# Four blocks on one core: the first half group ahead of the rest, its causal mask by a matrix product, fillers in TensorE's pauses, block 4's weights later, and separate buffers for the two feed-forward weights

## The chip, the core and the metric

The kernel runs on one NeuronCore of a Trainium2 chip. A core has TensorE (PE in the profile, with its weight loads as PEld), VectorE (DVE), ScalarE (ACT), GpSimd (POOL) and SyncE (SP), which here issues all DMAs. Each engine works through its own list of instructions in order; semaphores order them against each other. The metric is the device time of one execution in microseconds. Three runs of the kernel before gave 2677.88, 2680.63 and 2684.55, median 2680.63.

## The reference, cut to what matters

The input is x of shape [8, 1024, 256] in f32: 8 sequences of 1024 rows. Four blocks follow each other, each as `x = x + block(layernorm(x))`:

```python
x = x + _L0_attn_ref(_layernorm(x), ...)   # linear attention layer, own FFN 256-1024-256
x = x + _L0_ffn_ref(_layernorm(x), w1, b1, w2, b2)         # relu FFN 256-1024-256
x = x + _L1_attn_ref(_layernorm(x), W_qkv, b_qkv)          # softmax attention, one head
x = x + _L1_ffn_ref(_layernorm(x), w_gate, w_up, w_down)   # gated FFN 704 wide, fp4 inputs
```

Block 1, the linear attention, has 16 heads of 16 columns. With q and k after a sigmoid (so all entries are positive), and cumulative sums along the sequence:

```python
sink_in  = normal / einsum('bhld,bhld->bhl', q + EPS, cumsum(k, 2) + EPS)
src_out  = normal / einsum('bhld,bhld->bhl', k + EPS, cumsum(q, 2) + EPS)
cons_sink = einsum(..., q + EPS, cumsum(k * src_out[..., None], 2) + EPS) / normal
cons_src  = einsum(..., k + EPS, cumsum(q * sink_in[..., None], 2) + EPS) / normal   # then clip, exp
x = einsum('bhld,bhldm->bhlm', qs, cumsum(einsum('bhld,bhlm->bhldm', k, vs), 2)) * sink_alloc[..., None]
```

After it come an output product, a layernorm, a GELU feed-forward net and a second layernorm. In block 4 inputs and weights are quantized to fp4 in blocks of 16 values and widened again before each product.

## The kernel before, in words

**Tiling.** Rows are taken in chunks of 128, four chunks in a group (`G`), two groups in a sequence, so there are 64 chunks and 16 groups. All products are f32. Linear attention works by groups: `linear_group(p)` normalizes four chunks (`front`) and starts `linear_span`, which makes q and k, the running sums (scans on VectorE), the sums over heads (products `prod,hsum`) and `scale`; then `linear_chunk` handles each chunk: the product of k and q (`qz`, PSUM banks of 512 columns for four heads each), the causal mask, the product with v (`sc,v_pad`), the running state `kv`, the output product (`wo,xo`) and layernorm. The first group alone is done as two half groups (`spans` of chunks 0 to 1 and 2 to 3), which spread a packed per-head factor over columns by products with a mask (`spread_near`, tiles `flow` and `scale` times `mask`); all other groups spread it by a DMA to memory and back (`packed`, `spread`).

The causal mask of a chunk is a VectorE multiplication of each bank with an upper triangle, `sc = bank * triu`, four for each chunk.

**Feed-forward nets.** `dense()` runs over the groups; in a group first the GELU net on rows `hT`, then the ReLU net on rows `nT`, each for two halves of 256 rows and eight slices `f` of the 1024 hidden columns. One step is a first product (`half,w_ff`, two matmuls of 256 columns), the activation on ScalarE (`hidden`), and, `LAG = 2` steps later, the second product (`w_ff,hidden`), which adds into a bank of its half. There are 512 such steps. The weights of a step come from memory each time: `load_weights` issues, for each step, one DMA for the slice of the first weight and one for the slice of the second, into the two halves of one buffer `w_ff` of 512 columns; `W_FF = 5` such buffers exist, and one is free again after the second product of its step. After a half's last step `norms_1` or `norms_2` follows.

**Softmax and fp4.** `softmax_and_fp4` starts `soft_chunk` for each chunk of a sequence that is fully through block 2: scores (`n2T,qT`), exp, transposes, value product (`vt,probT`), normalization, fp4 quantization of 256 columns, gate and up products, fp4 quantization of 704 columns, down product (`wdT,hqT`), output DMA. `fp4_weights` quantizes block 4's weights in 18 pieces (`w_raw`) with the same VectorE steps.

**What sets the order.** Every part is a generator that yields what it needs next (engine, tiles, banks, a condition, and `at`, a due time in units of a group). `Plan.run` keeps a model of when each engine and tile is free, and at each turn takes the part with the smallest key: time that TensorE would wait, then how unripe it is, then engine, and last the due time. Instructions are pinned in the order in which they are issued (`Queue.issue`, so nearly all of the profile's instructions bear one line, L331). The order is thus fixed when the program is built; at run time nothing is reordered.

```python
wait = max(max(t) - now - (0.3 if stays else 0.0), 0.0)
unripe = max(t[1] + self.RIPE[queue] - now, 0.0)
key = wait, unripe, queue == "tensor", not stays, part[2]
```

Of the kernel before, what the change touches and what calls it, by code (L numbers as in the profile page):

```python
# [29 lines left out]
G = 4  # L30
# [32 lines left out]
class Plan:  # L63
# [12 lines left out]
    def __init__(self, tc, nc):  # L76
# [17 lines left out]
        self.ran = self.slow = 0.0  # L94
        self.parts = []
# [63 lines left out]
    def took(self, queue, op, args, kw):  # L159
# [13 lines left out]
        if queue == "tensor":  # L173
# [5 lines left out]
            if tiled:  # L179
                cost *= 0.25  # L180
# [80 lines left out]
    def act(self, *tiles, **kw):  # L261
        return self.need("scalar", tiles, **kw)
# [27 lines left out]
    def run(self):  # L290
        while self.parts:
            now = self.free.get("tensor", 0.0)
            best = None
            for part in self.parts:
# [5 lines left out]
                wait = max(max(t) - now - (0.3 if stays else 0.0), 0.0)  # L300
                unripe = max(t[1] + self.RIPE[queue] - now, 0.0)
# [3 lines left out]
            assert best is not None, "every part waits for another"  # L305
            if best[0][0] > 0.0 or best[1][1].queue == "tensor":
                self.free["tensor"] = max(now, best[2])
# [42 lines left out]
def block_stack_kernel(ctx: ExitStack, tc: tile.TileContext, a: dict, out: bass.AP):  # L350
# [138 lines left out]
    mask_tiles = [make("prob", "mask") for _ in range(2)]  # L489
    late = set()  # L490

    def masks():
        yield act(ident, at=0.02)
        for b in range(4):
# [12 lines left out]
    def late_constants():  # L507
# [10 lines left out]
        late.add("hsum")  # L518
        yield dve()
# [153 lines left out]
    def fp4_weights():  # L673
# [15 lines left out]
        for i, (src, turns) in enumerate(pieces):  # L689
            for j in range(i, min(i + 3, len(pieces))):  # L690
                if j not in raws:
# [3 lines left out]
                        dma(at=1.5 + 1.6 * i / len(pieces), when=lambda: count["stage"] == 4),  # L695
# [7 lines left out]
            at = 1.5 + 1.6 * i / len(pieces)  # L703
# [187 lines left out]
    def linear_group(p):  # L891
# [34 lines left out]
        for i in range(G):  # L926
            plan.start(front(i), p + 0.03 * i)
# [19 lines left out]
    def linear_span(p, span, fronts, tiles):  # L947
# [13 lines left out]
        after = 0.25 if span.start else 0.0  # L961
        near = len(span) < G

# [145 lines left out]
    def linear_chunk(p, i, n0T, comp, qk):  # L1109

        s, g = divmod(p, NG)
        past, c = seqs[s]["past"], p * G + i
        here = slice(i * P, (i + 1) * P)
# [6 lines left out]
        for k in range(2):  # L1120
# [25 lines left out]
                at=p + 0.62 + 0.06 * i,  # L1146
# [7 lines left out]
        qz = tile_qz.rearrange("p (k e t) -> p k e t", k=2, e=2)  # L1154
        for e in range(2):
# [4 lines left out]
        yield pe(qz, banks=4, tiled=True)  # L1160
        banks = []
        for r in range(4):
            rows = slice(32 * r, 32 * r + 32)
            bank = mm_bank()
            banks.append(bank)
            for k in range(2):
# [4 lines left out]
                    start=True,  # L1171
                    stop=True,
                )
        plan.drop(tile_qz)
        scores = []
        for bank in banks:
            sc = yield from fresh("flow", dve(bank), "sc")
            sc = sc.rearrange("p (n t) -> p n t", n=4)
            nc.vector.tensor_tensor(
# [7 lines left out]
        if not end:  # L1187
            yield pe(banks=1, at=p + 0.66 + 0.06 * i, when=lambda: count["attended"] == c)
# [77 lines left out]
        yield pe(xo, banks=1, at=p + 0.7 + 0.06 * i, when=lambda: "chunk" in late)  # L1266
        bank = mm_bank()
        for k in range(2):
# [14 lines left out]
            at=p + 0.74 + 0.06 * i,  # L1283
# [373 lines left out]
```

## Time and profile before

| what | before |
|---|---|
| median of three runs | 2680.63 us |
| profiled execution, its own time | 2684.53 us |
| its span, first to last instruction | 2682.8 us |
| PE busy / DVE busy / ACT busy | 2600.5 / 1937.8 / 1253.2 us |
| mean granted TensorE clock | 0.988 |
| VectorE mask `sc<-bank,triu`, 256 times | 160.6 us, 679 ns each |
| first-layer weight and second-layer weight DMAs | 1024 of 128 KB |
| table loads on ACT | 298, 1283 ns each |

Columns of the views: in the windows a line gives start:end of a stretch, its length, then for each engine the busy time and number of instructions, the granted clock as a share of full speed, the DMA engines' share and GB/s. In the timeline a line gives start, duration, engine, source line, operation, the tiles written and read, how many like instructions were merged, and in brackets the idle time just before and what ended it. An f32 product is two records on TensorE. A granted clock of 0.5 means that the same product takes twice as long. In the first 15 us the record of the clock is missing and the column shows 1.00.

### The profile page before, as it was taken

The page shows a single profiled execution, that of the slowest core. Times are in us where ns is not written, and L with a number is a line of the kernel's source. Part 1 is how long each engine was busy: PE and PEld are TensorE (multiplying, and loading weights), DVE is VectorE, ACT ScalarE, POOL GpSimd, SP SyncE. Part 2 cuts the span into 40 slices and gives each one's busy share as a digit, 9 for nine tenths or more (in the row PEclk, how much of TensorE's full clock was granted, in tenths as well). Part 3 has the DMA queues.
Part 4 walks back from the last instruction along what each step waited for, and adds up shares of the span by engine and source line. Part 5 has one row for each costly group of instructions (what it writes and reads, how often), then busy time and mean ns, then how long its engine had stood idle before and what let it go on. Part 6 is the DMA issues. An engine that isn't in the chain of part 4 may idle for free.

```text
span 2682.8 us, 45525 instructions
## 1 busy us (share of the span) xinstructions
PE 2600.5 (97%) x16687; PEld 2020.7 (75%) x16687; DVE 1937.8 (72%) x4368; ACT 1253.2 (47%) x2600; POOL 585.4 (22%) x1101
## 2 busy tenths in 40 slices
PE   6999999999999999999999999999999999999997
PEld 4777777777777877777777777777777777787765
DVE  7788786776858768586776858668586777855565
ACT  3444445546454453544445454453545435445342
POOL 1332222131212213132221212213122221212000
PEclk8899999999999999999999999999999999999999
DMA  3334232322223232232323223132322313222000
GB/s 87 98 107 142 79 95 74 95 70 86 70 81 105 69 87 66 75 107 64 103 62 89 72 77 109 60 89 70 93 77 72 103 58 87 74 75 81 28 16 8
DMA packets 286814, 211.88 MB, mean 79 GB/s; under 512 B 24704, under 2 KB 275072, under 8 KB 286592
## 3 DMA queue, kind: packets, MB, share of 16 engines
q1 hardware_dynamic: 286592, 208.97, 26.7%
q8 instruction: 133, 2.18, 0.3%
q14 instruction: 89, 0.73, 0.1%
HBM read 188.17 MB, written 20.71 MB: 78 GB/s over the span
## 4 chain that ended last, share of the span: by engine, by line
PE 81%; DVE 12%; DMA 3%; ACT 2%; issue 1%; POOL 1%; SPq 0%; DVEq 0%; ACTq 0%; POOLq 0%
PE bank L331 81%; DVE hid L331 1%; DVE prod L331 1%; DMA spread<-packed 1%; DVE n L331 1%; ACT L331 1%; DVE ln_st L331 1%; DVE x_amax L331 1%; DVE div L331 1%; DVE res L331 1%; DVE u L331 1%; DMA packed<-scale 1%; DVE q L331 0%; DVE ln_mv L331 0%; POOL ln_rstd L331 0%
## 5 line engine op out<-in xcount | busy, mean ns | idle before, releaser
L331 PE MATMUL bank<-half,w_ff 128*128 128x256 f32 x2048 | 535.5, 384 | 15.1 <-DMA w_ff<-in_L_ffn_w_dram 7.7
L331 PE MATMUL bank<-w_ff,hidden 128*128 128x256 f32 x2048 | 532.9, 384 | 0.0
L331 POOL TENSOR_SCALAR ln_ve<-ln_mv 128x1 f32<-128x1 f32 x384 | 103.3, 269 | 1747.3 <-DVE ln_mv L331 1739.3
L331 PEld LDWEIGHTS bank<-half,w_ff 128*128 128x128 f32 x2048 | 379.8, 191 | 93.3 <-issue 24.8
L331 PEld LDWEIGHTS bank<-w_ff,hidden 128*128 128x128 f32 x2048 | 370.6, 191 | 88.5 <-issue 39.1
L331 ACT ACT_TABLE_LOAD x298 | 382.3, 1283 | 5.2
L331 ACT ACTIVATE hidden<-bank,c_L_ffn_b 128x256 f32<-128x256 f32 x256 | 120.8, 472 | 298.9 <-PE bank L331 298.9
L331 POOL TENSOR_TENSOR ln_rstd<-ln_ve,neghalf 128x1 f32<-128x1 f32 x384 | 237.5, 619 | 32.0
L331 PE MATMUL bank<-n2T,qT 128*128 128x512 f32 x512 | 242.1, 596 | 1.1 <-ACT qT L331 1.1
L331 PE MATMUL bank<-vt,probT 128*128 128x256 f32 x1024 | 232.0, 380 | 0.0
L331 PEld LDWEIGHTS bank<-vt,probT 128*128 128x128 f32 x1024 | 193.3, 190 | 32.9 <-issue 2.9
L331 ACT ACTIVATE hidden<-bank,c_L_attn_b 128x256 f32<-128x256 f32 x256 | 119.7, 468 | 193.6 <-PE bank L331 192.9
L331 DVE TENSOR_TENSOR hid<-hid,bank 128x352 f32<-128x352 f32 x118 | 60.9, 516 | 199.0 <-PE bank L331 165.4
L331 PE MATMUL bank<-wdT,hqT 128*128 128x256 f32 x768 | 177.8, 381 | 0.8 <-ACT hqT L331 0.8
L331 PE MATMUL bank<-wgT,xqT 128*128 128x352 f32 x512 | 174.9, 464 | 0.6 <-ACT xqT L331 0.5
L331 PE MATMUL bank<-wuT,xqT 128*128 128x352 f32 x512 | 172.4, 459 | 0.0
L331 DVE TENSOR_TENSOR sc<-bank,triu 128x512 f32<-128x512 f32 x256 | 160.6, 679 | 13.0 <-PE bank L331 12.0
L331 PEld LDWEIGHTS bank<-wdT,hqT 128*128 128x128 f32 x768 | 144.5, 191 | 22.9 <-issue 1.7
L331 PEld LDWEIGHTS bank<-n2T,qT 128*128 128x128 f32 x512 | 94.3, 191 | 71.7 <-issue 61.3
L331 PEld LDWEIGHTS bank<-wuT,xqT 128*128 128x128 f32 x512 | 97.5, 190 | 54.5 <-issue 0.5
L331 PEld LDWEIGHTS bank<-wgT,xqT 128*128 128x128 f32 x512 | 95.2, 191 | 36.8 <-issue 1.9
L331 PE MATMUL bank<-ident,n 128*128 128x128 f32 x512 | 93.7, 278 | 21.8 <-DVE n L331 14.5
(213 smaller groups left out, 4363.8 us busy)
## 6 DMA issues: line engine op xcount, KB each, us to landing
w_ff<-in_L_attn_W_dram SPq DMA_DIRECT2D x512, 128.0 KB
w_ff<-in_L_ffn_w_dram SPq DMA_DIRECT2D x512, 128.0 KB
spread<-packed SPq DMA_DIRECT2D x90, 256.0 KB
x<-in_L_attn_inputs_dram SPq DMA_DIRECT2D x64, 128.0 KB
xr<-in_L_attn_inputs_dram SPq DMA_DIRECT2D x64, 128.0 KB
rows<-res SPq DMA_DIRECT2D x64, 128.0 KB
out_dram<-y SPq DMA_DIRECT2D x64, 128.0 KB
rows<-rows SPq DMA_DIRECT2D x56, 128.0 KB
```

Source lines behind the costliest of these rows:

```text
L331: ins = method(*args, **kw)
```

## The change

Six edits.

1. *First half group first.* The parts of chunks 0 and 1 of the first group get due times lowered by 1, which makes them negative; the planner calls a negative due time urgent: such a part counts as ripe at once. `after`, which is added to the due times of a span, becomes -1.0 for the first span of the first group; for the second it stays 0.25.
2. *The mask by a product.* In the first group a bf16 tile `later` holds (triu - 1) times 2 to the 100th, four times over, and an identity. A bf16 product of the two is written to each score bank first, and the scores are added to it; ScalarE's Relu then copies the bank to `sc`. Masked entries come out as zero. This replaces the VectorE multiplication in four chunks, 16 times. `later` takes one of the two `q_c` tiles until the last chunk of the first group is done.
3. *Fillers.* Where the planner's model has TensorE pause for more than 1.6 us, products of the identity with itself are put into the list ahead of the next instruction, one for each 0.22 us of the pause less 0.7.
4. *Block 4's weights later.* The due times of the 18 pieces go from 1.5 + 1.6 i/18 to 2.0 + 2.5 i/18.
5. *Softmax chunks later.* Their due times go from 3 + cc/4 to 3.5 + cc/4.
6. *Separate buffers.* The first weights go to tiles `w_in`, the second to `w_out`, five each of 256 columns, loaded by two generators; a `w_in` is free after its first product, a `w_out` after its second.

```diff
-                wait = max(max(t) - now - (0.3 if stays else 0.0), 0.0)
-                unripe = max(t[1] + self.RIPE[queue] - now, 0.0)
+                wait = max(max(t) - now - (0.3 if stays or part[2] < 0.0 else 0.0), 0.0)
+                urgent = part[2] < 0.0
+                unripe = 0.0 if urgent else max(t[1] + self.RIPE[queue] - now, 0.0)
                 key = wait, unripe, queue == "tensor", not stays, part[2]
                 if best is None or key < best[0]:
                     best = key, part, max(t)
             assert best is not None, "every part waits for another"
+            pause = max(now, best[2]) - self.ran
+            if pause > 1.6 and best[1][1].queue == "tensor" and self.fill is not None:
+                if (self.banks_free(best[1][1].banks + 1) or 0.0) <= self.ran + 0.4:
+                    self.fill(pause - 0.7)
...
+    later = make("q_c", "later")[:, : GT + P]
...
+        nc.scalar.copy(later[:, GT:], ident)
...
+        yield dve(triu)
+        nc.vector.tensor_scalar(
+            later[:, :GT].rearrange("p (n t) -> p n t", n=4),
+            triu.unsqueeze(1).to_broadcast([P, 4, P]),
+            -1.0,
+            2.0**100,
+            ALU.add,
+            ALU.mult,
+        )
...
-                        dma(at=1.5 + 1.6 * i / len(pieces), when=lambda: count["stage"] == 4),
+                        dma(at=2.0 + 2.5 * i / len(pieces), when=lambda: count["stage"] == 4),
...
-            plan.start(front(i), p + 0.03 * i)
+            plan.start(front(i), p + 0.03 * i - (p == 0 and i < 2))
...
-        after = 0.25 if span.start else 0.0
         near = len(span) < G
+        after = 0.25 if span.start else -1.0 if near else 0.0
...
+        at = p - (p == 0 and i < 2)
...
+        by_act = p == 0
         for e in range(2):
             nc.scalar.activation(
                 qz[:, :, e, :], qk[0][:, :, here], AF.Copy, scale=parity[:, e : e + 1]
             )
 
-        yield pe(qz, banks=4, tiled=True)
-        banks = []
-        for r in range(4):
+        yield pe(qz, *([later] if by_act else []), banks=4, tiled=not by_act)
+        banks = [mm_bank() for _ in range(4)]
+        for bank in banks:
+            if by_act:
+                nc.tensor.matmul(
+                    bank, lhsT=later[:, GT:], rhs=later[:, :GT], start=True, stop=False,
+                    skip_group_check=True,
+                )
+        for r, bank in enumerate(banks):
             rows = slice(32 * r, 32 * r + 32)
-            bank = mm_bank()
-            banks.append(bank)
             for k in range(2):
                 nc.tensor.matmul(
                     bank[:, k * D : (k + 1) * D],
                     lhsT=qk[1][rows, k, here],
                     rhs=qz[rows, k, :, :],
-                    start=True,
+                    start=not by_act,
                     stop=True,
+                    skip_group_check=True,
                 )
         plan.drop(tile_qz)
         scores = []
         for bank in banks:
-            sc = yield from fresh("flow", dve(bank), "sc")
+            sc = yield from fresh("flow", (act if by_act else dve)(bank), "sc")
             sc = sc.rearrange("p (n t) -> p n t", n=4)
+            if by_act:
+                nc.scalar.activation(sc, bank.rearrange("p (n t) -> p n t", n=4), AF.Relu)
+                scores.append(sc)
+                continue
...
-        def load_weights():
+        def load_weights(names, used, loaded, first):
+
             ws, n = [], 0
             for p in range(flows):
-                for wa, wb in (("L0_attn_W1", "L0_attn_W2"), ("L0_ffn_w1", "L0_ffn_w2")):
+                for name in names:
                     for f in 2 * list(range(NF)):
                         yield dma(
-                            at=p + 0.9 + n % 32 / 32,
-                            when=lambda: n < W_FF + seconds[0] and count["stage"] >= 2,
+                            at=p + 0.9 + (n % 32 + (0 if first else LAG)) / 32,
+                            when=lambda: n < W_FF + used[0] and count["stage"] >= 2,
                             unused=ws[n - W_FF :][:1] if n >= W_FF else (),
                         )
-                        w = big.tile([P, 2 * D], F32, tag="w_ff", name="w_ff", bufs=W_FF)
+                        tag = "w_in" if first else "w_out"
+                        w = big.tile([P, D], F32, tag=tag, name=tag, bufs=W_FF)
                         cols = slice(f * P, (f + 1) * P)
-                        nc.sync.dma_start(
-                            out=two(w[:, :D]), in_=a[wa][:, cols].rearrange("(k p) n -> p k n", p=P)
-                        )
-                        nc.sync.dma_start(out=w[:, D:], in_=a[wb][cols, :])
+                        if first:
+                            nc.sync.dma_start(
+                                out=two(w), in_=a[name][:, cols].rearrange("(k p) n -> p k n", p=P)
+                            )
+                        else:
+                            nc.sync.dma_start(out=w, in_=a[name][cols, :])
                         ws.append(w)
                         loaded.append(w)
                         n += 1
 
-        loaded, seconds = [], [0]
-        plan.start(load_weights(), 0.9)
+        firsts, seconds = [0], [0]
+        w_in, w_out = [], []
+        plan.start(load_weights(("L0_attn_W1", "L0_ffn_w1"), firsts, w_in, True), 0.9)
+        plan.start(load_weights(("L0_attn_W2", "L0_ffn_w2"), seconds, w_out, False), 0.9)
...
-                        behind.append((p, b, half, f, hidden, w))
+                        firsts[0] += 1
+                        behind.append((p, b, half, f, hidden))
...
-                at=3 + cc / 4,
+                at=3.5 + cc / 4,
...
+    def fill(us):
+
+        bank = mm_bank()
+        while us > 0.0:
+            nc.tensor.matmul(bank[:, :P], lhsT=ident, rhs=ident, start=True, stop=True)
+            us -= 0.22
+        plan.let_go(bank)
+
+    plan.fill = fill
```

## The prediction

> **What bounds the kernel.** I read the page first: busy shares, the slices, the chain that ended last.
>
> ```profile
> PE 2600.5 (97%) x16687; PEld 2020.7 (75%) x16687; DVE 1937.8 (72%) x4368; ACT 1253.2 (47%) x2600; POOL 585.4 (22%) x1101
> ...
> PEclk8899999999999999999999999999999999999999
> ...
> PE 81%; DVE 12%; DMA 3%; ACT 2%; issue 1%; POOL 1%; SPq 0%; DVEq 0%; ACTq 0%; POOLq 0%
> ```
>
> TensorE is the bound, and the chain is mostly TensorE work. But busy is not useful here: the first slices run below full clock. So I asked for busy time by stretch, cut at the first feed-forward product (76), at the transposes of `scale` in the second and third group (149, 256), at the last feed-forward product (2501) and at the last chunk's value product (2641).
>
> ```profile
> 0.00:76.00 76.00, 49.60 (x351) 36.20 (x352) 56.56 (x145) 23.82 (x65) 16.56 (x43) 0.80 0.30 77
> 76.00:149.00 73.00, 68.94 (x488) 54.91 (x488) 56.45 (x120) 30.62 (x74) 22.32 (x41) 0.95 0.41 115
> 149.00:256.00 107.00, 98.53 (x739) 78.47 (x738) 87.67 (x210) 46.60 (x115) 31.12 (x58) 0.94 0.41 119
> 256.00:2501.00 2245.00, 2226.11 (x14443) 1738.67 (x14442) 1623.80 (x3638) 1086.92 (x2214) 508.01 (x940) 1.00 0.28 81
> 2501.00:2641.00 140.00, 132.41 (x581) 95.50 (x579) 92.03 (x218) 57.28 (x117) 6.69 (x18) 0.99 0.05 17
> 2641.00:2683.00 42.00, 24.89 (x92) 16.93 (x90) 21.27 (x42) 7.95 (x16) 0.74 (x2) 0.88 0.03 10
> ```
>
> Columns: length, busy of PE, PEld, DVE, ACT, POOL, granted clock, DMA share, GB/s. Between 256 and 2501 nothing is to be had; the losses lie at the two ends. To size them I priced each product at its start-to-start spacing at full clock (216 ns for a record of 256 columns, two records per product; 109 for a transpose) and counted the records of each stretch. All work comes to 2531 us of the 2683; 152 are lost: 72 before 268 us, 46 between 268 and 2479, 34 after. The timeline shows their kinds:
>
> ```profile
> 49.56 4.14 PE L331 MATMUL bank<-qz,k 32*128 32x256 f32 x32
> ...
> 75.51 1.69 PE L331 MATMUL bank<-half,w_ff 128*128 128x256 f32 x4
> ...
> 129.67 2.07 PE L331 MATMUL bank<-half,w_ff 128*128 128x256 f32 x4 [3.75 <-DMA w_ff<-in_L_ffn_w_dram]
> ...
> 160.10 2.11 PE L331 MATMUL bank<-qz,k 32*128 32x256 f32 x16 [3.73 <-ACT qz L331]
> ...
> 237.22 2.07 PE L331 MATMUL bank<-half,w_ff 128*128 128x256 f32 x4 [3.11 <-DMA w_ff<-in_L_ffn_w_dram]
> ...
> 2674.11 1.51 PE L331 MATMUL bank<-ident,q 128*128 128x128 f32 x6 [7.28 <-DVE q L331]
> ```
>
> Four `half,w_ff` records take 2.07 us after a pause and 1.03 otherwise (90.72): each pause costs itself and some 3.4 us of halved rate. The queue that loads weights shows why two pauses are DMA:
>
> ```profile
> 120.38 0.89 SPq L331 DMA_DIRECT2D w_ff<-in_L_ffn_w_dram  x2
> 121.44 2.55 SPq L331 DMA_DIRECT2D spread<-packed  x4
> 124.09 1.04 SPq L331 DMA_DIRECT2D w_ff<-in_L_ffn_w_dram  x2
> ```
>
> The next pair stands behind `spread`, four transfers of 256 KB, and its product starts only at 129.67.
>
> **What the Trainium skill says.** "TensorE: Matmul & The Clock Gate", part 1 (What's actually happening): the clock is halved after an idle window of about 3.4 us and freed by a busy one, the windows running freely. The trace agrees: 42.5 to 52.8 and 66.4 to 76.7 run at clock 0.50, three windows each. Same page, Back-to-back issue gap: an isolated 512-column single-pass product takes N/2.4 + 2.5, some 216 ns; before has no bf16 product, so this is the only price. "ScalarE: Activation LUTs", Table sets: relu is in every set, so the new Relu should load no table; no run shows it yet.
>
> **The change, part by part.** Sums are made against the profiled execution: span 2682.8, its own time 2684.5; the median, 2680.6, is 3.9 lower.
>
> *Added TensorE work.* 16 mask products at 216 ns: 3.5 us. 141 fillers of 128 columns f32, two records of about 108 ns: 30.5 us at full clock. They cost nothing if they stand in real pauses: that is what must be checked. In the built order they stand in runs of 29, 6, 19, 11, 15 and 18 at the start, 6, 10, 14 and 13 at the end.
>
> *First half group first.* I follow the new order with old durations. `ident` is written by 3.04, so the 29 fillers start at 3.1; the first 3.4 to 6.8 us are at half clock: 6.3 + 1.7 to 3.4 = they end at 11 to 13, where `n` (now ahead of `rpos` and `same` on DVE, ready about 8.5) went through at 9.15. That is 2 to 3 us late, but at full clock: `k` reaches DVE at about 14.5, as before (14.38). Then the old run loses what the new order avoids: `wk` of the second half sat between `flow` and its mask products (22.98 to 26.35 on DVE): 3 us; second-half scans among the first's: 3 us. So first `weighted` at 22.5 (26.35), twelve DVE rows of 7 us and a carry wait of 1 to 30.5, head sums 0.7, `e` at 31.2 (37.51), then 4.7 (5.6 before, with the second half's `r` and `flow` inside): `scale` at about 36 instead of 43.1. At full clock what follows it shrinks (43.28 to 53.64 was half rate): scores out at 41 to 43. Eight Relus at about 0.6 (nearest row: ACT `prob` 128x512, 0.683; DVE's `sc` is 0.679) put attention at 45; `kT`'s copy stands behind seven of them, counted. Then `xo` 46.6, `wo` 47.6, `u` 48.8 (behind five rows of the second half), `h` of chunk 0 at 51; chunk 1's share the queue with 2.5 us of second-half rows: 55.8. The transposes and their copy end near 57: first feed-forward product at 57 against 75.5.
>
> *What that buys.* By the order lists 27.3 us of work precede that product before, 24.6 after. By the second group's `scale` it is 91.0 at 149.2, so 58 lost. After, the work is 94.2, and DVE sets the time: its rows up to there sum to 107.0 before and 107.8 after (16 `sc` of 0.62 gone, four more pieces of block 4's weights come earlier, 2.6 each). With DVE idle 15 us until 57 and 11 later: 134, so 40 lost. Bounds: no later idle 122, its old idle share 142. From there to the third group's `scale` before takes 107.2 for 89.6 of work; after 90.3 of work, no DMA pause (3.1, and 3.4 of halved clock), a shorter wait for `qz` (18 fillers hold the clock) and small waits: 96, bounds 92 and 107. Third `scale` at 230 instead of 256.4: 26 us gained, mask products included; bounds 7 and 42.
>
> *Separate buffers.* The same bytes and issues: five of 512 columns become five and five of 256. A first-layer weight comes free two steps earlier (the lag), 3.5 us at 1.73 a step. In SP's new order five `w_in` of the second network stand ahead of `spread`, three of them ahead of `packed`, where before had one pair, so the pause at 124.9 goes; it lies in the DVE-bound stretch, so it is in the 26, not on top. SP is in order and each `w_out` now waits alone; behind one stand `spread` and `xr`, for which DVE waits, as it did with pairs. Nothing to add.
>
> *Block 4's weights later.* Only the last ones move: the final piece from step 69 of the first products to 92, but eight pieces stand by step 18, where before had three. DVE between the third and fourth `scale` falls from 88 to 72 against TensorE's 108 and 98: hidden. One `q_c` buffer is held for the mask until the first group is done; Square waits behind DVE anyhow.
>
> *15 more table loads* at 1.283: 19 us of ACT, hidden under TensorE (ACT is 47% busy); uncovered, 1.3 us before a hidden tile each.
>
> *End.* Softmax chunks run half a group later; 181 us of work remain after the last feed-forward product against 148. Before, from the last value product's end (2641.1) to the last `y` (2680.0) 38.9 us pass for 19.6 of work, since the last two chunks share DVE and the last products run halved. In the new order the previous chunk's products fill its start: 2.6 + 4.7 of products, 3.0 of fillers, `n` at 10.8, products 4.7 to 16.3, transposes and `wdT` of the previous chunk to 20.3, last quantization 6.7 on DVE to 23.6, then 4.6: 28.2. Gain 10; bounds 5 (fillers 3 us late, one more wait) and 13. The stretch before it lost 11.6 for 128 of work; 162 at the same rate lose 14: 2 back. Middle: 46 lost, 23 of it in pauses under 1.9 us, 8 either way, taken as 0.
>
> Sum: 2684.5 - 26 - 10 + 2 = 2650.5; less 3.9: 2647.
>
> **Rivals.** (1) *DVE gives it back.* More pieces early stand in front of the second group's chain; TensorE runs out of feed-forward steps and waits. For it: DVE is 50 of 67 busy there, and a run of 18 fillers stands before that `scale`. Against: 16 `sc` are gone. Start gains 13, end 4: 2664. (2) *More than the ends.* `w_in` earlier also takes small waits of the middle, DVE without idle: start 36, end 12, middle 6: 2632. Against: DMA is only 0.8 of the waits after 268. (3) *Fillers delay work.* They are in order; one in front of a ready product costs itself. The 98 of the start at half rate are 42 us, the 43 of the end 9: if no pause were there, 2647 + 51 = 2698. It decides when 34 of these 51 hit ready work (no gain), 42 for slower. Against: TensorE idles 26 of the first 76 us. (4) *The clock stays halved* although filled: then only idle is rearranged, 2658; it lies within (1) and the forecast.
>
> **Numbers.** 0.3% (8 us, 2672.6 to 2688.6) is what a measurement tells from no change. Forecast 2647, own range 2636 to 2660: 0.60. (1) 2660 to 2672: 0.18. (2): 0.10. Within 0.3%: 0.05. (3), slower: 0.07. Faster 0.88. The range 2628 to 2668 leaves out half of (2), a third of (1) and the rest.
>
> **What would show it.** Right: first `w_in` product at 52 to 62; second and third `scale` transposes at 128 to 140 and 222 to 240; no `w_in` DMA pause over 2 us before 268; clock near 1.0 from 15 to 160; 28 us from the last value product to the last `y`; middle 46 lost. Wrong: fillers at 3 us ending after 14, products ready behind a run, `sc` Relus over 0.7, or DVE idle with TensorE idle before 250.

## The result, and the profile after

The changed kernel takes 2675.27 us (median of 13 runs, 2673.53 to 2677.35), the kernel before 2683.25 in the same session (13 runs). The ratio is 0.9971, with a 95% interval from 0.9963 to 0.9978: 8 us faster, where 34 had been forecast. The profiled span is 2674.1 us against 2682.8.

From the page of the changed kernel: busy time by engine, the granted clock in 40 slices, and the chain that ended last.

```profile
PE 2616.3 (98%) x16985; PEld 2040.7 (76%) x16985; DVE 1943.5 (73%) x4353; ACT 1282.5 (48%) x2641; POOL 566.3 (21%) x1101
...
PEclk9999999999999999999999999999999999999999
...
PE 67%; DVE 25%; DMA 3%; ACT 2%; issue 2%; POOL 1%; SPq 0%; DVEq 0%; POOLq 0%; ACTq 0%
```

Averaged over each slice, the clock is near full everywhere now. The chain is 67% TensorE where it was 81%, and 25% VectorE where it was 12%. That share says where the chain runs and not that TensorE waits longer: over the whole kernel its waits for VectorE sum to 37.8 us, where they were 56.9. They moved, as will be seen, from the ends into the middle. The same stretches as before (the last one ends with the shorter span):

```profile
0.00:76.00 76.00, 65.64 (x558) 55.81 (x559) 55.06 (x147) 35.78 (x97) 14.07 (x39) 1.00 0.37 93
76.00:149.00 73.00, 67.15 (x504) 52.57 (x503) 64.10 (x147) 32.15 (x76) 26.98 (x47) 0.98 0.42 119
149.00:256.00 107.00, 104.06 (x803) 84.23 (x803) 89.57 (x216) 49.34 (x120) 35.35 (x68) 1.00 0.46 131
256.00:2501.00 2245.00, 2215.32 (x14357) 1726.36 (x14357) 1616.98 (x3581) 1093.15 (x2211) 483.24 (x930) 1.00 0.28 80
2501.00:2641.00 140.00, 136.71 (x628) 100.25 (x627) 100.14 (x230) 66.30 (x127) 5.91 (x16) 1.00 0.05 16
2641.00:2674.00 33.00, 27.43 (x143) 21.50 (x141) 17.67 (x35) 5.73 (x12) 0.74 (x2) 1.00 0.04 13
```

The reader is to see two things. VectorE is busy 64 of the 73 us from 76 to 149 (56 before). And in the middle stretch, where nothing was expected to move, TensorE is busy 11 us less in the same 2245. The lines that answer to those of before, from the timeline of the changed kernel:

```profile
42.05 1.17 PE L337 MATMUL bank<-qz,k 32*128 32x256 f32 x16
...
60.61 1.13 PE L337 MATMUL bank<-half,w_in 128*128 128x256 f32 x4 [0.46 <-ACT half L337]
...
130.38 1.13 PE L337 MATMUL bank<-half,w_in 128*128 128x256 f32 x4
...
163.46 1.17 PE L337 MATMUL bank<-qz,k 32*128 32x256 f32 x16
...
2663.02 3.06 PE L337 MATMUL bank<-ident 128*128 128x128 f32 x26
2666.61 0.87 PE L337 MATMUL bank<-ident,hid 128*128 128x128 f32 x6 [0.53 <-DVE hid L337]
```

The first feed-forward product comes at 60.6 instead of 75.5, the DMA pauses at 129.67 and 237.22 are gone, so is the `qz` pause at 160, and before the last chunk's transposes stand fillers instead of 7.28 us of idle time.

Where the time went is counted as in the forecast. The lost time of a stretch is its length less the price of its TensorE records, and the price of a record is its start-to-start spacing at full clock in the kernel before; fillers count as lost. The stretches are cut at the transposes of `scale` of the third, fifth and sixteenth group.

| lost, us | to 3rd | 3rd to 5th | 5th to 16th | after 16th | two groups, steady |
|---|---|---|---|---|---|
| before | 73.2 | 11.1 | 32.4 | 37.1 | 320.6 |
| changed | 56.8 | 5.2 | 52.5 | 27.2 | 324.6 |

Below, "start" is the first of these columns, "middle" the third and "end" the fourth. The last column is the mean time of two groups between the eighth and the sixteenth. The start gains 16.4, of which the mask products take some 3.4 back: the third `scale` comes at 243.9 instead of 256.4 (230 was forecast). Groups four and five give 6 more, the end gives 10. Then the steady middle takes 20 back. Kernels with the same written order up to the third `scale` lost 55.3 to 58.2 there: a difference of under 3 us in one profile means nothing.

### The profile page after: what moved, and what is told of

Read it like the earlier page. It is cut to its first block, busy times and chain, and to the rows that moved or that the text cites. A ratio compares the mean times of both kernels' runs of the same rounds, so it can differ in the third digit from the quotient of the medians.

```text
span 2674.1 us, 46660 instructions
## 1 busy us (share of the span) xinstructions
PE 2616.3 (98%) x16985; PEld 2040.7 (76%) x16985; DVE 1943.5 (73%) x4353; ACT 1282.5 (48%) x2641; POOL 566.3 (21%) x1101
## 3 DMA queue, kind: packets, MB, share of 16 engines
q1 hardware_dynamic: 286592, 208.97, 27.2%
## 4 chain that ended last, share of the span: by engine, by line
PE 67%; DVE 25%; DMA 3%; ACT 2%; issue 2%; POOL 1%; SPq 0%; DVEq 0%; POOLq 0%; ACTq 0%
PE bank L337 67%; DVE hid L337 4%; DVE prod L337 3%; DVE n L337 2%; DVE ln_st L337 2%; DVE u L337 1%; DMA spread<-packed 1%; DVE x_amax L337 1%; DVE res L337 1%; DVE spread L337 1%; DMA packed<-flow 1%; DVE ln_mv L337 1%; ACT L337 1%; DVE div L337 1%; DVE mx L337 1%
## 5 line engine op out<-in xcount | busy, mean ns | idle before, releaser
L337 PE MATMUL bank<-half,w_in 128*128 128x256 f32 x2048 | 529.7, 381 | 6.7 <-DVE kv L337 3.4
L337 PE MATMUL bank<-w_out,hidden 128*128 128x256 f32 x2048 | 532.4, 383 | 0.0
L337 PEld LDWEIGHTS bank<-w_out,hidden 128*128 128x128 f32 x2048 | 369.8, 190 | 97.1 <-issue 45.1
L337 PEld LDWEIGHTS bank<-half,w_in 128*128 128x128 f32 x2048 | 378.0, 190 | 78.2 <-issue 19.8
L337 DVE TENSOR_TENSOR sc<-bank,triu 128x512 f32<-128x512 f32 x240 | 149.5, 680 | 9.3 <-PE bank L337 7.7
L337 PEld LDWEIGHTS bank<-wgT,xqT 128*128 128x128 f32 x512 | 94.4, 190 | 40.6 <-issue 6.3
L337 DVE TENSOR_TENSOR hid<-hid,q_c 128x704 f32<-128x704 f32 x116 | 102.8, 886 | 2.5
```

The costliest lines, as they stand in the source:

```text
L337: ins = method(*args, **kw)
```

## What cost the middle

Theory 1: the softmax chunks' new due time. Theory 2: the split weight buffers. Theory 3: an order that the new start leaves behind. Each is one part undone in the changed kernel; the due time was also put alone into the kernel before.

**The due time undone.**

```diff
-        at = 3.5 + cc / 4
+        at = 3 + cc / 4        # and at the two places that start a chunk
```

> The changed kernel, softmax chunks due at 3 + cc/4 again instead of 3.5 + cc/4. Theory 1 (the due time that frees the tail puts the softmax chunks of the middle in worse places): groups 5 to 15 lose some 32 us of TensorE time beyond its work, as before, instead of 52; the tail loses 37 again instead of 27; time some 2665. Theory 2 (the split weight buffers cost the middle) and theory 3 (an order inherited from the start does): the middle keeps its 52, the tail loses 37; time 2685.

Measured: 2666.45 us, ratio to before 0.9931 (0.9915 to 0.9948). Middle 35.2, end 32.7, two groups 320.1. Theory 1 holds for the middle; at the end only half of the gain went away. Waits of TensorE between the fifth and the sixteenth `scale`, from the view of waits (total us, times, longest), first the changed kernel, then this one:

```profile
PE bank L337 <- DVE sc L337: 5.6, 6, 1.7
PE bank L337 <- DVE v L337: 3.9, 7, 1.0
PE bank L337 <- DVE res L337: 3.6, 3, 1.2
PE bank L337 <- DVE prod L337: 3.4, 5, 1.2
PE bank L337 <- DVE kv L337: 2.2, 2, 1.1
```

```profile
PE bank L337 <- DVE v L337: 6.0, 9, 1.3
PE bank L337 <- ACT prob L337: 2.6, 5, 0.9
PE bank L337 <- DVE sc L337: 1.7, 1, 1.7
```

These are short waits, under 2 us, for rows (single instructions of VectorE) of the attention (`sc`, `kv`), of the scans (`prod`) and of the norms (`res`). VectorE was at work for 3.3 us or more of the 4 us before every one: the row waited for stands behind other rows. All waits of the view sum to 24.2 us in the changed kernel, 12.1 in the one before and 14.2 here. Counted as spacing over the price, pauses of over 0.25 us sum to 32.7, 14.3 and 16.9, which is nearly the whole difference. They return at fixed distances: the 1.19 us before an `h` transpose at 849.7 come again at 1498.2 and 2147.7. The order that the planner writes repeats, every four groups in the changed kernel, every two in this one.

**The due time alone, in the kernel before.**

> The kernel before with one edit, softmax chunks due at 3.5 + cc/4 instead of 3 + cc/4. Theory A (the later due time lets the written order fall into a repeating order with more pauses at results of VectorE, whatever the rest): the middle loses 40 to 52 instead of 32.4, two groups take over 321.5 us instead of 320.6, the tail loses 31 to 33 instead of 37.1 (it has no fillers): 2687 to 2700. If it takes the new start and the split buffers as well: middle 32, tail 32, 2677 to 2680.

Measured: 2687.15 us, 1.0009 (1.0001 to 1.0018). Middle 47.7 (32.4), end 31.3 (37.1), two groups 323.5. The view of waits between the fifth and sixteenth `scale`:

```profile
PE bank L331 <- DVE v L331: 13.1, 16, 1.7
PE bank L331 <- DVE kv L331: 4.8, 4, 1.2
PE bank L331 <- DVE res L331: 1.2, 1, 1.2
```

The kernel before waits 8.5 us for `v` and not at all for `kv` or `res`. So the later due time costs 15 to 17 us of middle in both kernels, and gains 5 to 6 at the end.

**The weight buffers joined again** (the loader, its two `dma_start` into one `w_ff` of 512 columns, and `w[:, D:]` in the second layer, as before).

> The changed kernel with both layers' weights in one buffer and one loader again. Theory 2 (split buffers cost the middle): the middle loses 32 instead of 52 and the time falls to some 2655 to 2660. Theories 1 and 3: the middle keeps 50 or more, DMA pauses ahead of first-layer products come back in the first 268 us (one or two of 3 us and 3.4 us of halved clock each); time 2675 to 2685.

Measured: 2680.56 us, 0.9984 (0.9976 to 0.9991). Middle 45.8, two groups 323.0; but the start loses 62.6 and groups four and five 11.3. Theory 2 falls: without the split the kernel is slower. The middle does lose 6.7 less than in the changed kernel, but not the 20 that the theory asks for; from the seventh group on the products stand in the order of the kernel without precedence, which comes next. Waits of TensorE before 268 us, this kernel:

```profile
PE bank L337 <- ACT qz L337: 3.8, 1, 3.8
...
PE bank L337 <- DMA w_ff<-in_L_ffn_w_dram: 3.2, 2, 2.9
```

Neither line is there in the changed kernel: the split is what removed both the DMA pause and the `qz` pause.

**The precedence of the first half undone.**

```diff
-            plan.start(front(i), p + 0.03 * i - (p == 0 and i < 2))
+            plan.start(front(i), p + 0.03 * i)
-        after = 0.25 if span.start else -1.0 if near else 0.0
+        after = 0.25 if span.start else 0.0
-        at = p - (p == 0 and i < 2)
+        at = p
```

> The changed kernel without the precedence of the first half group (front, turns and the attention's due times as before); mask by a product, fillers, later weights, split buffers and later softmax stay. Theory 3 (the order that the start leaves behind costs the middle): the middle loses 32 instead of 52 although the first feed-forward product comes at 68 to 76: time 2660 to 2675. Theories 1 and 2: the middle stays at 50 or more and the first product 8 to 15 us later costs 4 to 15: 2679 to 2690.

Measured: 2669.75 us, 0.9942 (0.9927 to 0.9957), faster than the changed kernel. Start 60.1, middle 40.4, two groups 322.2; the second `scale` comes at 142.8 instead of 147.6, although the first feed-forward product is as late as before (75.5). From the second group on, the planner's rules are those of the changed kernel; only what it starts from differs. So theory 3 holds beside theory 1: at one and the same due time the middle falls into different repeating orders.

**Block 4's weights at their old due times** (1.5 + 1.6 i/n).

> The changed kernel with the due times of block 4's weights as before (1.5 + 1.6 i/n instead of 2 + 2.5 i/n). The written order of the first three groups is that of the changed kernel, and so is that of the middle from the tenth group on: start 57, middle 50 to 53, tail 27; only the third to ninth group differ, where more VectorE work may cost up to 6: 2674 to 2681. If the due times matter for the start: outside that.

Measured: 2675.57 us, 0.9966 (0.9952 to 0.9979); start 55.9, middle 51.9, end 27.2. These due times alone change nothing that can be measured.

**Other due times**, 2.5 and 4.

> The changed kernel with softmax chunks due at 2.5 + cc/4. If the middle's loss grows with the due time: two groups take under 320 us, the middle loses 25 to 33, the tail 33 to 38: 2660 to 2668. If 3 is a good place by chance: two groups take 322 to 326, 2672 to 2690.

> The changed kernel with softmax chunks due at 4 + cc/4. If the middle's loss grows with the due time: two groups take over 325 us, the middle loses 55 or more, the tail 22 to 27: 2678 to 2695. If 3.5 is a bad place by chance: two groups take 320 to 323, 2662 to 2672.

Measured: at 2.5 2718.39 us (1.0131, 1.0116 to 1.0146), middle 80.7, two groups 329.1; at 4 2684.18 us (1.0004, 0.9995 to 1.0012), middle 45.7, two groups 322.8, end 34.4. From 2.5 to 4 the middle loses 80.7, 35.2, 52.5, 45.7: neither earlier nor later is better as such. At 2.5 the waits are mainly for ScalarE (18.8 us for `prob`). What the due time does is to choose the repeating order: every two groups at 2.5 and 3, every four at 3.5, every six at 4. Why one order has more pauses than another is not shown.

## What held the start back

The forecast saw VectorE's rows as the bound up to the second `scale`, and put it at 134. It came at 147.6.

**No piece of block 4's weights before the first group's feed-forward is done.**

```diff
-                        dma(at=2.0 + 2.5 * i / len(pieces), when=lambda: count["stage"] == 4),
+                        dma(at=2.0 + 2.5 * i / len(pieces),
+                            when=lambda: count["stage"] == 4 and count["dense"] >= 1),
```

> The changed kernel in which no piece of block 4's weights is loaded or quantized before the first group's feed-forward is done (before: eight of them by then). Theory B (VectorE bounds the second group, and the pieces are what fills it): second `scale` at 132 to 140 instead of 147.6, the gain kept at the third; together with the repeating order of the kernel without first-half precedence, into which this one falls too, 2652 to 2660. If other things than the pieces set the second `scale` (145 or later): 2664 to 2668.

Measured: 2675.33 us, 0.9963 (0.9950 to 0.9976). VectorE works 23 us less up to the second `scale` (94.9 us instead of 118.0) and that comes only 4.7 earlier, at 142.9. So the sum of VectorE's rows was not the bound. Groups four and five then lose 18.2 instead of 5.2: the pieces fall due there, and the gain is given back. From the sixth group on its products stand in the same order as in the kernel without precedence (322.4 for two groups). A line of its VectorE timeline:

```profile
120.15 0.69 DVE L337 TENSOR_TENSOR spread<-k,spread 128x512 f32<-128x512 f32 x1 [7.08 <-DMA spread<-packed]
```

With its other rows gone, VectorE waits 7.08 us for the transfer of `spread` in the middle of the second group's chain. That chain starts at the first group's last `wo` product. The timelines show it with the `wk` product behind it; kernel before, then changed kernel:

```profile
91.59 1.03 PE L331 MATMUL bank<-wo,xo 128*128 128x256 f32 x4
92.45 1.88 PE L331 MATMUL bank<-n0T,wk 128*128 128x512 f32 x4
```

```profile
94.06 1.03 PE L337 MATMUL bank<-wo,xo 128*128 128x256 f32 x4
94.92 1.88 PE L337 MATMUL bank<-n0T,wk 128*128 128x512 f32 x4
```

In all twenty kernels the second group's first `wk` product starts 0.9 us after the fourth chunk's `wo` product of the first group. The code says why: `q` and `k` have one buffer, and line 990 holds these products back until `count["linear"] >= p * G`, which the `wo` products count. From there to `scale` it takes 50 to 57 us. Precedence for the first half sends the second half through later: its `scale` comes at 71.3 instead of 66.7 before (65.6 without precedence), and the fourth `wo` at 94.1 instead of 91.6 (89.9). What the first feed-forward product gains, 15 us, is not on this chain.

The buffer is not the whole of it. ScalarE writes `k` from the `wk` product, and the group's first running sum on VectorE (`prod<-one,carry_cur,k`) reads it. Both in the kernel before, then in the changed kernel:

```profile
94.37 0.69 ACT L331 ACTIVATE k<-bank,bqk 128x512 f32<-128x512 f32 x1 [0.81 <-PE bank L331]
95.39 1.28 DVE L331 TENSOR_TENSOR_SCAN prod<-one,carry_cur,k 128x512 f32<-128x512 f32 x1
```

```profile
96.84 0.69 ACT L337 ACTIVATE k<-bank,bqk 128x512 f32<-128x512 f32 x1 [2.25 <-PE bank L337]
105.75 1.27 DVE L337 TENSOR_TENSOR_SCAN prod<-one,carry_cur,k 128x512 f32<-128x512 f32 x1
```

Before, the sum starts 0.3 us after `k` is written, in the changed kernel 8.2 us after. Twenty VectorE rows are written ahead of it there: sixteen of the layer norms that follow the first group's `wo` products, four of block 4's weights. With block 4's pieces away it is still 6.6 us; without precedence it is 0.3 again. So VectorE does hold the second group back here, by the order of its rows and not by their sum. Further on, from `flow` to `scale`, 28 to 31 us pass in all twenty kernels, whether VectorE is busy for 20 of them or for 28. No run gives `q` and `k` a second buffer or puts the sums ahead of the norms, so what either would be worth is not shown.

**The mask on VectorE again.**

```diff
-        by_act = p == 0
+        by_act = False
```

> The changed kernel with the first group's mask on VectorE again (16 mask products of TensorE and the Relus of ScalarE gone, 16 `sc` rows of 0.62 us on VectorE back). Theory A (the middle's loss is that of the repeating order into which the written program falls; from the tenth group on this kernel's TensorE order is word for word that of the kernel without first-half precedence and of the joint-buffer kernel): two groups take 322.2 us in the middle instead of 324.5, the middle loses 40 to 45 instead of 52.5. Theory B (VectorE bounds the second group): its `scale` comes later than 147.6, at 152 to 158. Both together 2670 to 2676; A without B 2663 to 2667; B without A (middle unchanged) 2680.

Measured: 2680.84 us, 0.9981 (0.9974 to 0.9989). The second half's `scale` comes at 76.3, the second group's at 151.3, 75.0 later (76.3 later in the changed kernel): the chain again, started later. Start 64.2, middle 41.2 with 322.2 for two groups, and from the tenth group on its products are written in the same order as those of the kernel without precedence. Theory A holds. Theory B does not: the second `scale` is later, but less than it asked for, and its distance from the second half's has not grown. The end loses 34.2, which was not foreseen. Its written order is another one there, and after the sixteenth `scale` TensorE waits 5.7 us for ScalarE's exponentials written to `flow` and 4.1 for those in `prob`, where the kernel without precedence waits 0.8 and 2.4.

**The second group's first layer norms let go earlier** (at due time 3).

```diff
+        early = range(2) if p == 1 else ()
+        for i in early:
+            plan.start(front(i), p)
         yield dve(at=p, when=lambda: count["v"] == p * G)
...
-            yield pe(n0, banks=1)
+            yield pe(n0, banks=1, when=lambda: n0T is not None)
```

> The changed kernel with softmax chunks due at 3 + cc/4, and the layer norms of the second group's first two chunks no longer behind the last `wv` product of the first group (only the rows that follow them still are). Theory C (the second group's `scale` comes a fixed 73 to 77 us of serial work after that of the second half group, whatever VectorE has to do beside it; that work starts when the second half's `wv` products are through): second `scale` 3 to 6 us earlier than the 148.2 of the same kernel without this edit, 2660 to 2664 if it is kept to the end. Theory B (VectorE's sum sets it): second `scale` at 147 to 149, time 2666.

Measured: 2670.28 us, 0.9944 (0.9930 to 0.9959): slower than due time 3 alone. The second `scale` comes 75.3 after the second half's; kernels with the changed kernel's start have 75.2 to 76.9. The layer norms were not what the chain waits for, since the `wk` product still follows the fourth `wo`; the theory had the chain right and its first link wrong. The third `scale` does come 3.4 us earlier than with due time 3 alone (241.0 against 244.4), little more than the spread of equal orders, and it is not kept: moving the rows cost 10.0 between the fifth and the sixth group, where due time 3 alone loses 3.8.

## What the fillers are worth

```diff
-    plan.fill = fill
```

> The changed kernel without the 141 fillers (30.5 us of TensorE time at full clock). If they stand in real pauses and hold the clock, as the forecast has it: halved clock comes back for some 10 to 25 us of the first 150 us and of the last 40, each costing half of the work in it: 2680 to 2690. If they delay ready work (third rival): 2650 to 2672. If the pauses are idle anyway and the clock matters little: 2675 within 3.

Measured: 2683.31 us, 0.9995 (0.9989 to 1.0002), that is 6.5 us more than the changed kernel in the profiled span. The end loses 32.7 instead of 27.2 and the start 60.0 instead of 56.8, with the clock at half from 30.4 to 40.6, 57.7 to 64.5 and 2655.2 to 2662.0, among others. The written order of the real work is the same, so this is their own value. It is a balance: without fillers the first half's `scale` comes at 34.9, with the changed kernel's fillers at 36.9 to 39.1, since `n` is there at 7.0 and its transposes stand behind the first run of fillers until 12.3 (7.04 without). The halved clock takes more than that back by the third `scale` (246.9 against 243.9). Its timeline at the end:

```profile
2655.80 0.66 PE L337 MATMUL bank<-ident,n 128*128 128x128 f32 x2 [3.59 <-DVE n L337]
2656.91 2.72 PE L337 MATMUL bank<-wgT,xqT 128*128 128x352 f32 x4 [0.46 <-ACT xqT L337]
2659.42 2.55 PE L337 MATMUL bank<-wuT,xqT 128*128 128x352 f32 x4
```

The same place with fillers:

```profile
2649.59 3.29 PE L337 MATMUL bank<-ident 128*128 128x128 f32 x28
2653.34 0.41 PE L337 MATMUL bank<-ident,n 128*128 128x128 f32 x2 [0.46 <-DVE n L337]
2654.21 1.45 PE L337 MATMUL bank<-wgT,xqT 128*128 128x352 f32 x4 [0.46 <-ACT xqT L337]
```

The pause is filled but for 0.46 us, and the products after it run in 1.45 us instead of 2.72.

## Looking for both gains

The later due time is good for the end and bad for the middle, so it was tried late only.

**Due time 3, and 3.5 for the last sequence.**

```diff
-        at = 3.5 + cc / 4
+        at = (3.0 if cc < 56 else 3.5) + cc / 4   # and at the two other places
```

> The changed kernel with softmax chunks due at 3 + cc/4, but those of the last sequence (cc from 56) at 3.5 + cc/4. Theory (the later due time helps only by what it leaves for the end, and harms only by the repeating order of the middle): middle 35 as with all at 3, tail 27 instead of 32.7: 2659 to 2662. If the end's gain needs the later time of all chunks: tail 32 to 33, 2665 to 2667.

Measured: 2667.38 us, 0.9930 (0.9914 to 0.9947), middle 36.1, end 33.3: no gain, the second case of the expectation. The value products of eight chunks are left when the feed-forward ends, as with 3; with 3.5 throughout those of eleven are.

**The same with block 4's weights after the first group,** and softmax chunks only when those weights are ready:

```diff
-... and "softmax" in weights and "ends" in late,
+... and "softmax" in weights and "fp4" in weights and "ends" in late,
```

> Both together (no piece of block 4's weights before the first group's feed-forward is done; softmax chunks due at 3 + cc/4, the last sequence's at 3.5 + cc/4; a softmax chunk starts only when block 4's weights are ready, without which the two would wait for each other). If the gains add: second `scale` at 132 to 140, middle 33 to 35, tail 27: 2648 to 2655. If the late pieces gain nothing: 2660. If they push their work into the third and fourth group at TensorE's cost, as the pause that they avoid: 2660 to 2670.

Measured: 2677.22 us, 0.9967 (0.9956 to 0.9978). Second `scale` at 143.2, but 15.9 lost from the third to the fifth group and 11.3 in the next: the late pieces are paid for there. That is the third case of the expectation.

**Due time 3 without precedence, with that rule; then the rule alone.**

> The changed kernel with softmax chunks due at 3 + cc/4 and without the precedence of the first half group (softmax chunks start only when block 4's weights are ready, without which the two would wait for each other). If the precedence costs only through the repeating order that the middle falls into: the middle loses 33 to 36 as with precedence, the start 60 instead of 57: 2667 to 2671. If it costs in itself (the second half and with it the second group later): 2658 to 2664.

> The changed kernel with softmax chunks due at 3 + cc/4 that start only when block 4's weights are ready; precedence kept. If that rule is what cost 20 us in the kernel without precedence (all of it lost in the third to fifth group): 2682 to 2688, groups 3 to 5 losing 25 to 31 instead of 10.7. If the missing precedence cost it: 2665 to 2669.

Measured: 2686.55 us (1.0008, 0.9999 to 1.0017) without precedence and 2663.99 us (0.9924, 0.9908 to 0.9941) with it. The rule itself costs nothing; it takes 3.7 us out of the middle (31.5), since the groups after the fifth fall into the good order at once. Without precedence this kernel loses 18.1 from the third to the fifth group and 13.1 in the next, and its first value product comes at 435 us instead of 360. So precedence is worth 22.6 us here and cost 5.5 at due time 3.5: neither is a property of precedence, and neither expectation had it.

**Due time 3.5 from the sixth sequence on** (`cc < 40`).

> The changed kernel with softmax chunks due at 3 + cc/4 up to the fifth sequence and at 3.5 + cc/4 from the sixth (cc from 40). If the end's gain needs only that ten or eleven chunks are left when the feed-forward ends: middle 36 to 39, tail 27 to 28, 2660 to 2664. If not, 2666 to 2669.

Measured: 2660.82 us, 0.9916 (0.9902 to 0.9931), middle 35.5, end 27.4, the value products of ten chunks left. This is what the forecast's end was worth without its price.

**With the rule that softmax waits for block 4's weights; and with the earlier layer norms.**

> The changed kernel with softmax chunks due at 3 + cc/4 up to the fifth sequence and 3.5 + cc/4 from the sixth, and started only when block 4's weights are ready. If the two gains add: start 57, middle 32, tail 27.4: 2656 to 2660. If the tail pays for the rule (35.2 against 32.7 with due time 3 alone): 2660 to 2664.

> The same with the layer norms of the second group's first two chunks ahead of the second half's last `wv` product. Theory C (chain from the second half's end): second `scale` 2 to 4 us earlier after the second half's `scale`; if the rows so moved do not upset the groups that follow, 2653 to 2657; if they do, as at due time 3 without the rule (10 lost in one group), 2660 to 2668.

Measured: 2657.53 us (0.9904, 0.9887 to 0.9920) and 2658.98 us (0.9908, 0.9893 to 0.9923). The first loses 56.5, 6.6, 31.8 and 27.5 in the four stretches: the gains add. The earlier layer norms bring nothing in the end: the second `scale` comes 74.8 after the second half's, against 76.1, and the third at 240.1, against 243.6, but the sixteenth at 2242.3, against 2240.2. The faster kernel is 26 us under the kernel before and 18 under the changed one, by two edits to when softmax chunks may go. It is the best of several orders tried, so it does not show that the same edits would help another kernel.

## Why the prediction was wrong

The direction was right, the size was not: 2647 with 2628 to 2668, measured 2675. In profiled executions it is 2650.5 against 2675.9, 25.4 us too few: some 13.6 up to the second `scale` and 14.2 from the third `scale` to the sixteenth, less 1.9 that the end gained beyond the forecast. (The rest is the correction to the median: three runs had put the kernel before at 2680.6, thirteen put it at 2683.25.) Point by point:

- *The start* was right up to the first feed-forward product: fillers from 3.10 to 12.46 (11 to 13), `scale` of the first half at 38.1 (36), mask products 0.216 us apart (0.216), Relus of 0.5 in a run and 0.64 alone (0.6), first feed-forward product at 60.6 (57). The eight Relus run without a table load between them, as the Trainium skill has it ("ScalarE: Activation LUTs", Table sets).
- *"With DVE idle 15 us until 57 and 11 later: 134"* is the first step that failed: 147.6. Taken as a sum it was short in both terms: VectorE is busy 118.0 us up to there, where it had 107.8, and idle 29.6, where it had 26. For the kernel before, its own two lines of busy time give 113.0, where the sum of rows had 107.0. But the sum was also the wrong bound: 23 us of rows less brought 4.7. What sets the stretch is a chain from the fourth `wo`, and on it the place of the rows: the first running sum waits 8.2 us behind other rows. Two signs were to be had in the kernel before: VectorE was idle 36.0 of its first 149.2 us, and the `wk` product at 92.45 stood right behind the fourth `wo`. The change moved that `wo` later, not earlier.
- *From the second to the third `scale`*, 96 was forecast and 96.3 measured. The DMA and `qz` pauses went, as the sum had it, and the joined buffers bring them back.
- *"Middle: 46 lost, 23 of it in pauses under 1.9 us, 8 either way, taken as 0"* is the second step that failed. Groups four and five gained 5.9, the eleven after lost 20.1. The bounds of 8 looked at the pauses there were, not at those that a new order can have; the term was put at nothing although the due time of every softmax chunk moved. The edit with the least code in it, a due time moved by half a group, had its price there: 17 us of the 20 go when it is undone.
- *The end*: from the last value product to the last `y` 28.9 us (28.2 forecast, 38.9 before). Right in size, and by the mechanism named: more chunks left, and fillers. Of the 9.9 that the end as a whole gained, 5.5 go without the fillers, and 5.5 with the old due time.
- *Fillers cost nothing*: right on balance. They are worth 6.5 us, after the delay at the start, which the forecast had too (2 to 3 us late). The clock was near full from 15 to 160 but for one window, 141.7 to 145.2; "TensorE: Matmul & The Clock Gate" of the skill, part 1, has windows of about 3.4 us, and this one is 3.4. The forecast had from the same page that a window has to be idle to halve the clock. This trace does not agree: in the 3.4 us before 141.7 TensorE was idle for only 1.4.

Of the rivals, the first (VectorE gives the start back) had the measured symptom, the second `scale` nearly as late as before, and part of its cause: taking block 4's pieces away brought 4.7 of the missing 13.6 us. The rows in front of the second group's chain were in the main the first group's own norms, which it did not name. None of the rivals had the middle lose.

## What to carry to other kernels

Where a planner writes the order of a long steady loop, price the loop and not only the ends: the smallest change to a due time can move it into another repeating order, and 2 us in each group outweigh what a start of 150 us can give. Before a sum of busy time is taken as the bound of a stretch, ask what its last result hangs on and which rows are written ahead of it: here the second group hung on the end of the first, and its first running sum stood behind twenty other rows. And where a late due time is wanted for the end of a kernel, set it for the end.

## What was not expected of the hardware

Some 24 us of pauses, each under 2 us, spread over the 1780 us of the middle did not lower the clock in the changed kernel: no slow window lies between 145 and 2674 us. But short pauses do not keep it safe. The slow window at 141.7 came after three pauses of 0.61, 0.66 and 0.76 us:

```profile
137.66 0.86 PE L337 MATMUL bank<-prod,hsum 128*32 128x128 f32 x24 [0.61 <-DVE prod L337]
138.46 1.13 PE L337 MATMUL bank<-w_out,hidden 128*128 128x256 f32 x4
140.25 0.44 PE L337 MATMUL bank<-ident,n 128*128 128x128 f32 x2 [0.66 <-DVE n L337]
141.44 0.38 PE L337 MATMUL bank<-total,front 128*128 128x1 f32 x2 [0.76 <-ACT e L337]
```

With joined buffers one came at 1797.4, after a pause of 1.58 us, while pauses of 1.72 us in the changed kernel brought none. What decides is not shown.

And one written order does not give one time: up to the first half's `scale`, fifteen kernels with the same order of products and fillers took 36.9 to 39.1 us, so that a single profile cannot tell a start that is 1 or 2 us better. The spread follows the clock. The first fillers change from half to full rate (records 213 and then 111 ns apart in the changed kernel) at some 6.0 us in the fastest of them and at 9.1 in one that takes 38.4: 3.1 us more at half clock for 1.5 us more at `scale`. The two slowest, both 39.1, have besides a slow window from about 21.7 to 25.1, which the others have not.
